# Moving the weighted sum of key products behind the next tile's key eviction on VectorE

## The chip, the cores and the metric

The kernel runs on one core of a Trainium2 chip. A core has a matrix engine (TensorE, PE in the profile; its weight loads are PEld), three elementwise engines (VectorE or DVE, ScalarE or ACT, GpSimd or POOL), a queue that issues transfers (SyncE or SP) and 16 DMA engines. Each engine works through its own instructions in the order in which they stand, and waits for another engine only through semaphores. The metric is the device time of one execution in microseconds (us); lower is better.

## What is computed

One block of a transformer with adaptive layer norms: an attention-like layer, then a mixture of experts, both with residuals. Only the first is touched here. For each of 2 sequences of 1024 tokens of width 512:

```python
h = layernorm(x) * (1 + ca) + sa
Xn = layernorm(h, gamma, beta)
Q, K, V = split(Xn @ W_in + b_in, 3)
K, V = rotary(K), rotary(V)                # on the first 256 of 512 columns
A = sum over tokens of K/|K| * V/|V|       # one row of 512 numbers per sequence
A = 0.5 * A + 0.5
y = (A * Q) @ W_out + b_out + h
x = x + ga * y
```

The row A needs all tokens of its sequence, so nothing of that sequence's output can be computed before its last tile has been added in. Then come a second norm, the choice of 2 of 8 experts for each token, the experts, a shared expert, and the residual. All is in float32.

## The kernel before

The 2048 tokens are 16 tiles of 128, tiles 0 to 7 for the first sequence and 8 to 15 for the second. A tile t passes through these steps:

- `norm1` (L343 to L366): both layer norms. VectorE does the statistics (L311, L312), the reciprocal (L315), the shift and scale (L353, L359) and the offset of the second norm (L322); ScalarE does the square root (L314) and the last scaling into `hn` (L323).
- `turn1` (L368): four transposes on TensorE (L328, `tr_a`), evicted by ScalarE into `xnT` (L375).
- `kv_half(t, 0)` and `kv_half(t, 1)` (L385): four matmuls each into one PSUM bank, keys for 0 and values for 1 (L391). VectorE evicts the bank and adds the bias into half of the tile `kv` (L398). The bank comes from a ring of three (`mm_ps`, L97), which other steps share.
- `kv_back(t, acc)` (L400): ScalarE takes the squares (L408) and the norms (L424). VectorE forms the product of keys and values, `pr` (L410), and the weight `w` = 1/(|K||V|) (L425, L427). GpSimd makes the rotary's part of the product from the same `kv` (L415 to L419); the last of its five instructions writes the tail of `pr`. Then VectorE adds w times `pr`, 768 columns, to the running sum `acc` (L429 for the first tile of a sequence, L431 for the others). That last instruction is the "weighted sum" of this case. The tile `pr` has two buffers, `w` three, `acc` one.

`mix` (L433) turns a finished `acc` into the row A: four small VectorE instructions (L437 to L440), four matmuls with one column (L443, `amix`), two small VectorE instructions. `one_matrix` (L471) folds A into the product of the query and output weights, wp (L496). `project(t, wp)` (L511) then multiplies tile t by it (L522, `o`) and adds the residual on VectorE (L516, L529, L530) and GpSimd (L519); `norm2` (L538) makes `hr` from it, by way of L311, L314, L315, L322 and L323, and `turn2` (L543) transposes `hr` (L328, `tr_c`), evicts it on ScalarE (L550) and scales `hr` on GpSimd (L558, L559).

The first loop (L1044) runs `norm1(t + 2)`, `kv_half(t, 0)`, `turn1(t + 1)`, some side work on the modulation vectors (`side`, L1018), `kv_half(t, 1)` and `kv_back(t)` for tiles 0 to 7. After `mix(0)` and `one_matrix(0)` a plan (L1102) and the list behind it (L1117) interleave `project` of tiles 0 to 7 with the same key and value steps of tiles 8 to 15, the first routing steps (`logits`, `choose`, `ranks`) and chunks of the shared expert. After tile 15 come `mix(1)`, `one_matrix(1)`, `project` of tiles 8 to 15, and from about 345 us on the experts.

The order in the text isn't quite that of the engines: when the program is built, a scheduler sets the order of the instructions on each engine, keeping what depends on what. `tc.issue_after(ins)` tells it to place the instructions of a block behind `ins` on the engine of `ins`.

Of the kernel before, what the change touches and what calls it, by code (L numbers as in the profile page):

```python
# [12 lines left out]
ALU = mybir.AluOpType  # L13
# [11 lines left out]
def kernel(  # L25
# [20 lines left out]
    nc = tc.nc  # L46
    B, S, D = x.shape
# [3 lines left out]
    NJ = S // P  # L51
# [45 lines left out]
    def mm_ps(name):  # L97
        return ps_mm.tile([P, 512], FP, tag="mm", name=name)

    def tr_ps(name):  # L100
        return ps_tr.tile([P, 512], FP, tag="tr", name=name)
# [83 lines left out]
    b_kv = epool.tile([P, 2 * D], FP, name="b_kv")  # L185
# [195 lines left out]
            )  # L381

    fronts = {}

    def kv_half(t, i):  # L385
        g, j = t // 4, t % 4
        if i == 0:
            fronts[t] = kvp.tile([P, 2, D], FP, tag="kv", name=f"kv_{t}")
        ps = mm_ps(f"kv_{t}_{i}")
        for k in range(KC):  # L390
            nc.tensor.matmul(  # L391
                ps,
                xnT[g][:, k, j * P : (j + 1) * P],
                w_kv[:, i, k, :],
                start=(k == 0),
                stop=(k == KC - 1),
            )
        nc.vector.tensor_add(fronts[t][:, i, :], ps, b_kv[:, i * D : (i + 1) * D])  # L398

    def kv_back(t, acc):  # L400

        kv = fronts.pop(t)
        ss = small.tile([P, 2], FP, tag="ss", name=f"ss_{t}")
        sq = kvp.tile([P, D], FP, tag="sq", bufs=1, name=f"sq_{t}")
        for i in range(2):
            nc.scalar.activation(sq, kv[:, i, :], AF.Square, accum_out=ss[:, i : i + 1])  # L408
        pr = kvp.tile([P, D + 2 * R2], FP, tag="pr", name=f"pr_{t}")
        nc.vector.tensor_mul(pr[:, 0:D], kv[:, 0, :], kv[:, 1, :])  # L410
        pair = kv[:, :, 0:ROT].rearrange("p w (i two) -> p w i two", two=2)
        prod = pr[:, 0:ROT].rearrange("p (i two) -> p i two", two=2)
        cross = kvp.tile([P, 2, R2], FP, tag="cross", bufs=1, name=f"cross_{t}")
        both = kvp.tile([P, 2, R2], FP, tag="both", bufs=1, name=f"dsum_{t}")
        nc.gpsimd.tensor_mul(cross[:, 0, :], pair[:, 0, :, 0], pair[:, 1, :, 1])  # L415
        nc.gpsimd.tensor_mul(cross[:, 1, :], pair[:, 0, :, 1], pair[:, 1, :, 0])
        nc.gpsimd.tensor_add(both[:, 0, :], cross[:, 0, :], cross[:, 1, :])
        nc.gpsimd.tensor_sub(both[:, 1, :], prod[:, :, 0], prod[:, :, 1])
        nc.gpsimd.tensor_mul(  # L419
            pr[:, D:].rearrange("p (w i) -> p w i", w=2), both, cs[:, t % NJ]  # L420
        )
        inv = small.tile([P, 2], FP, tag="inv", name=f"inv_{t}")
        nrm = small.tile([P, 2], FP, tag="nrm", name=f"nrm_{t}")
        nc.scalar.activation(nrm, ss, AF.Sqrt)  # L424
        nc.vector.reciprocal(inv, nrm)  # L425
        w = small.tile([P, 1], FP, tag="w", name=f"w_{t}")
        nc.vector.tensor_mul(w, inv[:, 0:1], inv[:, 1:2])  # L427
        if t % NJ == 0:
            nc.vector.tensor_scalar(acc, pr, w, None, ALU.mult)  # L429
        else:  # L430
            nc.vector.scalar_tensor_tensor(acc, pr, w, acc, ALU.mult, ALU.add)  # L431

    def mix(b, acc):  # L433

        pair = acc[:, 0:ROT].rearrange("p (i two) -> p i two", two=2)
        half = kvp.tile([P, 2, R2], FP, tag="cross", bufs=1, name=f"half_{b}")
        nc.vector.tensor_add(half[:, 0, :], pair[:, :, 0], pair[:, :, 1])  # L437
        nc.vector.tensor_add(half[:, 1, :], acc[:, D : D + R2], acc[:, D + R2 :])
        nc.vector.tensor_add(pair[:, :, 0], half[:, 0, :], half[:, 1, :])
        nc.vector.tensor_sub(pair[:, :, 1], half[:, 0, :], half[:, 1, :])  # L440
        ps = tr_ps(f"amix_{b}")
        for f in range(KC):
            nc.tensor.matmul(  # L443
                ps[:, f : f + 1],
                acc[:, f * P : (f + 1) * P],
                ones_t[:, 0:1],
                start=True,
                stop=True,
            )
        aT = small.tile([P, KC], FP, tag="aT", name=f"aT_{b}")  # L450
        RC = ROT // P
        nc.vector.tensor_scalar(
            aT[:, 0:RC], ps[:, 0:RC], 0.5 * (1.0 - HALF), HALF, ALU.mult, ALU.add
        )
        nc.vector.tensor_scalar(
            aT[:, RC:KC], ps[:, RC:KC], 1.0 - HALF, HALF, ALU.mult, ALU.add
        )
        return aT
# [543 lines left out]
    def start_acc(b):  # L1002
        return kvp.tile([P, D + 2 * R2], FP, tag="acc", bufs=1, name=f"acc_{b}")
# [39 lines left out]
    acc = start_acc(0)  # L1043
    for t in range(NJ):  # L1044
        if t == 0:
            norm1_mid(2)
            norm1_out(2)

            nc.vector.scalar_tensor_tensor(
                cs[:, :, 0, :], cs[:, :, 1, :], -2.0, cs[:, :, 0, :], ALU.mult, ALU.mult  # L1050
            )
            nc.vector.scalar_tensor_tensor(
                cs[:, :, 1, :], cs[:, :, 1, :], -2.0, cs[:, :, 1, :], ALU.mult, ALU.mult
            )
            nc.vector.tensor_scalar(cs[:, :, 1, :], cs[:, :, 1, :], 1.0, None, ALU.add)
        else:
            norm1(t + 2)
        kv_half(t, 0)
        turn1(t + 1)
        for step in side[t]:  # L1060
            step()
        kv_half(t, 1)
        kv_back(t, acc)
    kv_half(NJ, 0)
    turn1(NJ + 1)
    kv_half(NJ, 1)
    aT = mix(0, acc)
    norm1(NJ + 2)
    wp = one_matrix(0, aT)
# [24 lines left out]
    def ranks(g):  # L1094
# [5 lines left out]
    acc = start_acc(1)  # L1100
    T = NJ
    plan = {  # L1102
        0: [(kv_back, T, acc), (kv_half, T + 1, 0), (turn1, T + 2)],
        1: [(turn2, 0), (kv_half, T + 1, 1), (kv_back, T + 1, acc)],
        2: [(turn2, 1), (kv_half, T + 2, 0), (turn1, T + 3)],
        3: [(turn2, 2), (kv_half, T + 2, 1), (kv_back, T + 2, acc)],
# [10 lines left out]
    for step, *args in [  # L1117
# [26 lines left out]
        step(*args)  # L1144
    units.close()
    aT = mix(1, acc)
    early.close()
    gbp = ctx.enter_context(tc.tile_pool(name="gbp", bufs=1, reuse_waits="tile"))
# [458 lines left out]
```

## Time and profile before

| | |
|---|---|
| three runs | 793.36, 794.96, 795.88 us; median 794.96 |
| the profiled execution | 793.29 us; its span 791.5 us |
| granted TensorE clock, mean | 0.994 |
| PE busy | 759.0 us, 96% of the span |
| VectorE, ScalarE, GpSimd busy | 426.7, 233.3, 212.0 us |
| L391, matmuls of keys and values | 256 records, 115.3 us |
| L398, their eviction on VectorE | 32, of 658 to 692 ns |
| L431, the weighted sum | 14, of 1017 to 2007 ns |
| L429, the same for the first tile of a sequence | 2, of 611 and 620 ns |
| L419, GpSimd's last instruction before it | 0.72 to 1.05 us |

The span is from the first to the last instruction that the profiler saw; the time of the execution is 1.8 us longer. Percentages over the whole span hide that its stages differ: the keys and values are made from about 19 to 243 us, and the experts, a long stretch in which TensorE has almost no gaps, fill more than half of the rest. A float32 matmul leaves two records, so eight records of L391 are one `kv_half`. In the listing by time, a row gives the start, the duration, engine, line and operation, and in brackets how long the engine sat idle before it and what ended the wait.

### The profile page before, as it was taken

To read this page: it belongs to the slowest core of one execution; us is meant where nothing else is said; L and a number is where in the kernel's file an instruction comes from. 1 tells how busy PE (TensorE), PEld (TensorE's weight loads), DVE (VectorE), ACT (ScalarE), POOL (GpSimd) and SP (SyncE) were. 2 spreads that over 40 slices of the span, in tenths; PEclk is the share of its full clock that TensorE was granted. 3 is DMA by queue.
4 is the path that set the end of the run, shared out by engine and by line. 5 is a ranking of instruction groups with operands and counts; after the bars stand their busy time and mean duration, and the time that the engine had idled before them with its cause. 6 is when DMAs were issued, how large, how long until landed. Compare 5 with 4: busy or idle time off the path is not lost. (4 is left out here: it accounts for less than half of the span.)

```text
span 791.5 us, 8532 instructions
## 1 busy us (share of the span) xinstructions
PE 759.0 (96%) x2547; PEld 418.1 (53%) x2547; DVE 426.7 (54%) x980; ACT 233.3 (29%) x495; POOL 212.0 (27%) x241
## 2 busy tenths in 40 slices
PE   7989999998999978999999999999999999899997
PEld 2433444444444433477466565656566565688542
DVE  4887756788745378897122123323222121489965
ACT  4564532447633046121012112122121121122310
POOL 1233324853621387574200000000000000224530
PEclk9999999999999999999999999999999999999999
DMA  9940001211435520247999999999999976624551
GB/s 324 384 143 28 0 1 66 107 45 49 160 93 173 212 106 27 81 176 248 363 324 328 325 335 334 336 340 327 326 332 333 335 248 232 197 85 120 162 170 53
DMA packets 96369, 158.91 MB, mean 201 GB/s; under 512 B 8089, under 2 KB 51097, under 8 KB 96321
## 3 DMA queue, kind: packets, MB, share of 16 engines
q1 hardware_dynamic: 89984, 138.41, 51.7%
q0 software_dynamic: 5760, 18.88, 7.2%
q10 hardware_dynamic: 576, 1.05, 0.4%
q8 instruction: 22, 0.36, 0.2%
q14 instruction: 27, 0.21, 0.1%
HBM read 128.15 MB, written 30.16 MB: 200 GB/s over the span
## 5 line engine op out<-in xcount | busy, mean ns | idle before, releaser
L1259 POOL DMA_INDIRECT y<-ybuf,yrows x32 | 37.0, 1157 | 334.4 <-SPq L1485 287.1
L391 PE MATMUL kv<-w_kv,xnT 128*128 128x512 f32 x256 | 115.3, 597 | 4.6 <-DVE kv L398 2.5
L1385 PE MATMUL by<-wd_r,gtT 128*128 128x512 f32 (+1 forms) x210 | 96.1, 593 | 0.9 <-DVEq L1477 0.9
L1357 PE MATMUL bg<-wg_r,hbT 128*128 128x352 f32 x280 | 88.9, 460 | 0.9 <-ACT y L1389 0.9
L1357 PE MATMUL bu<-wu_r,hbT 128*128 128x352 f32 x280 | 88.5, 459 | 0.0
L391 PEld LDWEIGHTS kv<-w_kv,xnT 128*128 128x128 f32 x256 | 47.0, 190 | 62.0 <-issue 49.0
L1357 PEld LDWEIGHTS bu<-wu_r,hbT 128*128 128x128 f32 x280 | 53.2, 190 | 29.6
L1372 DVE COPY gtT<-gtr 128x256 f32<-128x256 f32 x35 | 14.9, 425 | 97.0 <-PE gtr L1369 97.0
L1357 PEld LDWEIGHTS bg<-wg_r,hbT 128*128 128x128 f32 x280 | 50.4, 190 | 23.5 <-ACT y L1389 1.3
L522 PE MATMUL o<-wp,xnT 128*128 128x512 f32 x128 | 58.4, 602 | 0.0
L1385 PEld LDWEIGHTS by<-wd_r,gtT 128*128 128x128 f32 (+1 forms) x210 | 37.2, 191 | 34.6 <-issue 33.5
L1236 DVE TENSOR_TENSOR sg_b<-sg_b,bg 128x352 f32<-128x352 f32 x35 | 18.2, 521 | 68.8 <-ACT sg_b L1235 68.8
L1349 ACT COPY hbT<-tr_b 128x512 f32<-128x512 f32 x36 | 21.1, 586 | 101.1 <-PE tr_b L328 101.1
L1237 DVE TENSOR_TENSOR gt<-sg_b,bu 128x352 f32<-128x352 f32 x35 | 18.3, 521 | 47.2 <-PE bu L1357 47.2
L1389 ACT COPY y<-by 128x512 f32<-128x512 f32 x35 | 20.5, 587 | 70.8 <-DMA wg_r<-in_w_gate_dram 35.7
L522 PEld LDWEIGHTS o<-wp,xnT 128*128 128x128 f32 x128 | 24.4, 195 | 29.2 <-issue 27.5
L573 POOL DMA_INDIRECT hbuf<-again,rows x24 | 25.6, 1068 | 50.5 <-DMA again<-hlin 24.3
L1235 ACT ACTIVATE sg_b<-bg 128x352 f32<-128x352 f32 x35 | 16.2, 464 | 76.1 <-PE bg L1357 76.1
L415 POOL TENSOR_TENSOR cross<-kv 128x128 f32<-128x128 f32 x16 | 12.7, 791 | 82.1 <-DVE kv L398 49.6
L408 ACT ACTIVATE sq<-kv 128x512 f32<-128x512 f32 x32 | 20.1, 629 | 35.0 <-DVE kv L398 31.2
L496 PE MATMUL wp<-aw,wqT 128*128 128x512 f32 x64 | 28.3, 597 | 0.9 <-DVE aw L480 0.8
L519 POOL TENSOR_TENSOR x<-x,sa 128x512 f32<-128x512 f32 x16 | 20.3, 1269 | 31.5 <-DVE sa L508 15.6
(315 smaller groups left out, 1269.7 us busy)
## 6 DMA issues: line engine op xcount, KB each, us to landing
wg_r<-in_w_gate_dram SPq DMA_DIRECT2D x35, 704.0 KB, 6.1
wu_r<-in_w_up_dram SPq DMA_DIRECT2D x35, 704.0 KB, 7.5
wd_r<-in_w_down_dram SPq DMA_DIRECT2D x35, 512.0 KB, 5.6
hb<-hbuf SPq DMA_DIRECT2D x36, 256.0 KB, 5.0
ybuf<-y SPq DMA_DIRECT2D x31, 256.0 KB, 5.4
wd_r<-in_w_down_dram SPq DMA_DIRECT2D x35, 192.0 KB, 5.4
wmod<-in_wmod_dram SPq DMA_DIRECT2D x6, 1024.0 KB, 9.9
x<-in_x_dram SPq DMA_DIRECT2D x3, 1024.0 KB, 10.5
```

Of the source, the lines that this page charges most:

```text
L391: nc.tensor.matmul(ps, xnT[g][:, k, j * P : (j + 1) * P], w_kv[:, i, k, :], start=(k == 0), stop=(k == KC - 1),)
L408: nc.scalar.activation(sq, kv[:, i, :], AF.Square, accum_out=ss[:, i : i + 1])
L496: nc.tensor.matmul(ps, wqT[:, k, f * P : (f + 1) * P], aw[:, k, :], start=(k == 0), stop=(k == KC - 1),)
L519: nc.gpsimd.tensor_add(xt, xt, sg[b])
L522: nc.tensor.matmul(ps, xnT[g][:, k, j * P : (j + 1) * P], wp[:, k, :], start=(k == 0), stop=(k == KC - 1),)
L573: ins = nc.gpsimd.indirect_dma_start(out=hbuf, out_offset=bass.IndirectOffsetOnAxis(ap=idx, axis=0), in_=src, in_offset=None, bounds_check ...
L1237: nc.vector.tensor_mul(dst, sg[:m, :n], pu[:m, :n])
L1259: nc.gpsimd.indirect_dma_start(out=y, out_offset=None, in_=ybuf, in_offset=bass.IndirectOffsetOnAxis(ap=yrows[:, t, s : s + 1], axis=0), b ...
L1349: nc.scalar.copy(hbT.rearrange("p k q -> p (k q)"), ps)
L1357: nc.tensor.matmul(ps[:, :H], hbT[:, k, :], wt[:, k, :], start=(k == 0), stop=(k == KC - 1))
L1385: nc.tensor.matmul(ps, gtT[:m, c, :], w[2][:m, c, :], start=(c == 0), stop=(c == NH - 1))
L1389: nc.scalar.copy(y, ps)
```

## The change

```diff
     fronts = {}
+    waiting = []
...
-        nc.vector.tensor_add(fronts[t][:, i, :], ps, b_kv[:, i * D : (i + 1) * D])
+        ins = nc.vector.tensor_add(
+            fronts[t][:, i, :], ps, b_kv[:, i * D : (i + 1) * D]
+        )
+        if i == 0 and waiting:
+
+            with tc.issue_after(ins.ins):
+                waiting.pop()()
...
-        if t % NJ == 0:
-            nc.vector.tensor_scalar(acc, pr, w, None, ALU.mult)
-        else:
-            nc.vector.scalar_tensor_tensor(acc, pr, w, acc, ALU.mult, ALU.add)
+
+        def accumulate():
+            if t % NJ == 0:
+                nc.vector.tensor_scalar(acc, pr, w, None, ALU.mult)
+            else:
+                nc.vector.scalar_tensor_tensor(acc, pr, w, acc, ALU.mult, ALU.add)
+
+        waiting.append(accumulate)
 
     def mix(b, acc):
 
+        if waiting:
+            waiting.pop()()
```

`kv_back` no longer issues the weighted sum; it leaves it in a list. The next `kv_half(t, 0)`, the keys of the next tile, issues it directly behind its own eviction. For the last tile of the second sequence there is no next tile, and `mix` issues it, where it stood before. No instruction is added or taken away.

What this makes of the order on the engines, in the built program:

| place | VectorE before | VectorE after |
|---|---|---|
| tile 1 | w, sum 1, offset (L322), keys 2, reciprocal | w, offset, reciprocal, keys 2, sum 1 |
| tile 3 | w, sum 3, keys 4, side step (L258), offset, reciprocal, side step | w, offset, keys 4, sum 3, two side steps, reciprocal |
| tile 7 | w, sum 7, keys 8, mix | w, offset, keys 8, sum 7, mix |
| tile 8 | sum 8 inside `one_matrix` | keys 9, sum 8 |
| tile 9 | w, sum 9, L529 to L322 of projection 2, keys 10 | w, L529 to L322 of projection 2, keys 10, sum 9 |
| tile 11 | w, reciprocal, sum 11, offset, L529 of projection 6 | w, reciprocal, offset, L529 of projection 6; the sum much later, behind keys 12 |

("keys t" is the eviction L398 of `kv_half(t, 0)`.) The other tiles go like these. TensorE keeps its order but for one tile: matmuls of `kv_half(2, 1)` and four groups of transposes of the query weights (L466) mix in another way. ScalarE has a few square roots, norms and evictions exchanged with their neighbours. GpSimd has one place, at tile 12, where the five instructions of L415 to L419 come ahead of two others (L999 and L1000) instead of between and behind them. SyncE keeps its order.

## Prediction

> **What bounds the kernel.** I read the page's busy line first, then the chain that ended last, then the list of who waited for whom on PE.
>
> ```profile
> PE 759.0 (96%) x2547; PEld 418.1 (53%) x2547; DVE 426.7 (54%) x980; ACT 233.3 (29%) x495; POOL 212.0 (27%) x241
> ...
> PE m L961 8%; PE sd L873 5%; PE ph L1244 1%; DVE spare_again L1288 0%; DVE spare_again L1289 0%
> ```
>
> TensorE is busy for 759.0 of 791.5 us and the chain's long pieces are TensorE's. No matmul is removed, so the change can win only gaps of TensorE: 32.5 us in all, and only those before the last weighted sum at 243.7 us that come from VectorE's order. By stretches of 10 us the granted clock is 1.00 as far as 250 us, so no clock is to be gained there. From 400 to 600 us PE is busy for 100.0 of each 100 us: work that starts earlier there should end earlier by as much.
>
> ```profile
> PE tr_c L328 <- ACT hr L323: 8.8, 7, 4.6
> PE kv L391 <- DVE kv L398: 2.5, 2, 1.7
> PE kv L391 <- ACT xnT L375: 2.1, 3, 1.0
> ...
> PE wqT L466 <- ACT xnT L375: 1.4, 1, 1.4
> ...
> PE amix L443 <- DVE acc L440: 1.2, 1, 1.2
> ```
>
> Columns: total us, times, longest. These five lines are my candidates; the largest wait of the first line, 4.6 us at 281, lies behind the last weighted sum (there L530 waits 5.4 us for GpSimd's L519) and is not one.
>
> **Where the wait sits.** VectorE by time, around tile 4:
>
> ```profile
> 62.82 0.16 DVE L312 BATCH_NORM_AGGREGATE mv<-st_a 128x2 f32<-128x6 f32 x1
> 64.54 1.02 DVE L431 SCALAR_TENSOR_TENSOR acc<-pr,w,acc 128x768 f32<-128x768 f32 x1 [1.56 <-POOL pr L419]
> 65.48 0.68 DVE L398 TENSOR_TENSOR kv<-kv,b_kv 128x512 f32<-128x512 f32 x1
> ```
>
> and TensorE in the same stretch:
>
> ```profile
> 55.16 7.13 PE L391 MATMUL kv<-w_kv,xnT 128*128 128x512 f32 x16 [0.81 <-DVE kv L398]
> 62.13 0.60 PE L328 MATMUL tr_a<-ident,hn 128*128 128x128 f32 x4
> 62.66 1.88 PE L252 MATMUL modsum<-wmod,pick 128*2 128x512 f32 x4
> 66.22 7.13 PE L391 MATMUL kv<-w_kv,xnT 128*128 128x512 f32 x16 [1.68 <-DVE kv L398]
> ```
>
> The keys of tile 4 were complete at about 62.2, but VectorE stood before the weighted sum of tile 3, which waited for GpSimd until 64.5, took 1.02, and only then evicted them. The bank was needed again (three banks, two of them with the side step), so TensorE stood 1.68 us. Over all weighted sums VectorE idled 15.2 us for L419, but a wait of VectorE costs only where TensorE stands behind it.
>
> **Part 1, the eviction goes in front (tiles 0 to 6).** No cost: the same instructions. The eviction takes 0.66 to 0.69 in all 32 cases and fills the wait (0.58 to 1.65 us a tile up to tile 7). At tile 4 it can start at 63.0 to 63.2 and end by 63.9, before TensorE wants the bank at 64.54; at tile 3 it ends by 54.1 (a statistic, 0.66, is now ahead of it too), wanted at 54.35. So the two waits of L391 go: 0.81 + 1.68 = **2.5 us**. Between: 1.7 if tile 3's bank is late, 2.5 at most.
>
> **Part 2, the offset no longer behind the sum.** At tile 1 the offset L322 ran at 42.72, after the sum; by the new order it can run at 40.8, so `hn` (42.97) and the three evictions of `xnT` behind it (to 44.83), which held TensorE for 1.39 us, come nearly 2 us sooner. But TensorE's own order there changes: two matmul records of the 8 now stand ahead of the transposes instead of four, so it arrives 0.95 us sooner. The two gaps there, 1.39 + 0.27, become about 0.9 + 0.35: gain **0.4**, bounds -0.3 and 1.4.
>
> **Part 3, `mix(0)`.** L443 waits 1.19 us for L440. If the sum of tile 7 still starts at 100.73, when L419 is done, the four instructions of `mix` no longer have the eviction (0.60 from start to start) ahead of them: 0.6. The earlier offset of tile 6 (94.11, now about 91.7) also frees the eviction of tile 7's values, at 96.36 although TensorE had finished them near 94.8; with it GpSimd's five start earlier. Taken **1.0**, at most 1.2.
>
> **Part 4, tiles 8 to 15.** The sum of tile 9 and what stood behind it:
>
> ```profile
> 137.81 0.25 DVE L427 TENSOR_TENSOR w<-inv 128x1 f32<-128x1 f32 x1
> 139.78 2.01 DVE L431 SCALAR_TENSOR_TENSOR acc<-pr,w,acc 128x768 f32<-128x768 f32 x1 [1.72 <-POOL pr L419]
> 141.72 0.73 DVE L529 SCALAR_TENSOR_TENSOR u<-u,rs,o 128x512 f32<-128x512 f32 x1
> ```
>
> L529 had its matmul at about 138.2, and waited 3.5 us in VectorE's queue. From L529 to `hr` (145.76) are 4.0 us, and `tr_c` stood 0.62 us for it. Now L529 starts near 138.3. The same holds at 154.93 (`tr_c` waits 0.36) and 172.72 (1.04). Sum 2.02. The moved sum takes 1.0 to 2.0 us behind the keys' eviction, where VectorE waited 1.5 to 3 us for `o` anyway; without that cover it would lengthen the next `hr` by as much.
>
> [...] What used to idle until L419 now runs L530 and L516, both with two SBUF inputs, against L419, L558 and L559. [...]
>
> ```profile
> 197.50 6.93 DVE L410 TENSOR_TENSOR pr<-kv 128x512 f32<-128x512 f32 x1
> ```
>
> It let six GpSimd instructions in a row pass: 6.3 us lost. By that row L530 would get in only after L559, near 142.4, where it ran before (142.49), and part 4 would bring nothing. [...] The eviction itself has one input in PSUM and showed no lengthening beside L519 at 145.64 and 150.75, so parts 1 and 3 don't hang on this.
>
> **Part 5, further down.** Because the offset at 174.65 no longer waits for the sum of tile 11, ScalarE's `hn` (174.88), then the exponential and its table loads up to 184.7 come 1.8 to 3.4 us sooner; TensorE, about 1 us sooner itself, stood 0.54 + 1.00 for `xnT` of tile 12: half of it, **0.7** (0 to 1.5). The wait of `lg` at 210.1 (0.63) follows the offset at 207.92, which also moves ahead of its sum: **0.3** (0 to 0.6). `mix(1)` gains nothing: its sum ends at 244.7, `amix` runs in TensorE's order at 249.7.
>
> Behind this, DMA waits on buffers that TensorE frees, and GpSimd's scatters wait for row numbers from the matmuls at 250.5; both move with TensorE. The sum: 2.5 + 0.4 + 1.0 + 1.7 + 0.7 + 0.3 = 6.6. I take off 1.0 for new small gaps where TensorE, now earlier, catches up with ScalarE (estimate: the size of one `xnT` wait): **5.6 us**. The profiled execution took 793.29 (span 791.5 and 1.8 around it), so 787.7; it lay 1.67 below the median of the three runs. Against the median: 794.96 - 5.6 = **789.4**.
>
> **Rivals.** A measurement tells 0.3%, 2.4 us, from no change.
>
> A, only the first stage gains (parts 1 to 3, 2.5 to 3.9 us; part 4 lost to GpSimd): about 791.5. [...] 20%.
>
> B, no effect: TensorE's gaps move. The per-tile chain norm, transpose, `xnT` is as long as TensorE's 8.8 us a tile, and what is won at 54 and 64 is lost at the next `tr_a`. Against: VectorE is busy 6.6 to 8.4 of each 10 us from 40 to 100, and `hn` at 66.90 is wanted at 73.2. Also here: the scheduler's other exchanges cost what the gaps bring. About 794.5. 17%.
>
> C, slower, one mechanism: GpSimd keeps VectorE out. If L530 or L516, now inside GpSimd's run, loses 6.3 us as L410 did, `hr` comes 6.3 - 3.5 = 2.8 us later than before. At the three places of part 4 that is 8.4, less the 3.9 of the first stage: 799.5. It is slower from about two such places on (5.6 against 3.9). For: the row. Against: GpSimd's runs there are three instructions, not six. 12%.
>
> The forecast has 51%, its own range 786.8 to 791. Faster by over 0.3% (below 792.6): 51 and most of A, 68%. Same: 20%, B and the weak end of A. Slower: 12%. For 8 in 10: from 786.8, all bounds at their good end, to 795, which takes in A and most of B.
>
> **What would show it.** Part 1: the list of PE's waits has no L391 waiting for L398. Part 2: less than 1.3 us at L466. Part 3: L443's wait below 0.4. Part 4: `tr_c` waits for `hr` no more between 140 and 190, and L530 stays below 2 us. Part 5: L391 waits for `xnT` less than 1 us. PE's idle time falls from 32.5 to about 27. I am wrong if L431's wait for L419 vanishes and PE's idle time stays, or if a VectorE instruction of several us stands in front of an `hr`.

## The result, and the profile after

The change makes the kernel faster, by more than was forecast. Six executions of the changed kernel have a median of **786.11 us** (783.34 to 788.17). Six of the kernel before, run beside them, have 796.14 (793.36 to 797.12). The ratio is 0.988, with a 95% interval of 0.985 to 0.991. The forecast was 789.4 us with a range from 786.8: the sign is right, the gain is too small, and the measured time lies 0.7 us below the range. Chance can have a part in those 0.7 us: when both kernels ran again (`e1_before` and `e2_after` below), the changed one had a median of 788.46, inside the range, and the gain by medians was 7.5 us instead of 10.0. That the parts of the sum were too small together isn't chance; the ledger below shows it place by place.

The profiled execution took 788.17 us, with a span of 786.2. The page's busy line:

```profile
PE 760.1 (97%) x2547; PEld 420.3 (53%) x2547; DVE 428.1 (54%) x980; ACT 232.6 (30%) x495; POOL 212.8 (27%) x241
```

TensorE has the same 2547 records and is busy for the same time within 1.1 us. Its idle time fell from 32.5 to 26.1 us, so most of the gain is in its gaps, as forecast. The list of who waited for whom on TensorE (engine, tile and line, released by; total us, times, longest):

```profile
PE tr_c L328 <- ACT hr L323: 6.9, 4, 4.5
PE kv L392 <- ACT xnT L375: 3.3, 2, 2.8
```

Of the five lines shown of before, those for `kv` behind VectorE's eviction, for `wqT` and for `amix` no longer occur, and `tr_c` went from seven waits to four. One line grew: `xnT` from 2.1 to 3.3. (The new lines 399, 426, 440, 542 and 543 are 398, 419, 431, 529 and 530 of before, and the matmul of keys and values is L392. The kernels of the experiments have line numbers of their own; the tile's name tells what a row is.)

VectorE and TensorE around tile 4, by time:

```profile
60.86 0.21 DVE L322 TENSOR_SCALAR off_b<-mv_b,rs_b 128x1 f32<-128x1 f32 x1
60.99 0.68 DVE L399 TENSOR_TENSOR kv<-kv,b_kv 128x512 f32<-128x512 f32 x1
62.47 1.02 DVE L440 SCALAR_TENSOR_TENSOR acc<-pr,w,acc 128x768 f32<-128x768 f32 x1 [0.80 <-POOL pr L426]
```

```profile
59.94 1.88 PE L252 MATMUL modsum<-wmod,pick 128*2 128x512 f32 x4
61.75 7.13 PE L392 MATMUL kv<-w_kv,xnT 128*128 128x512 f32 x16
```

The eviction of the keys (L399) stands ahead of the sum. VectorE still waits for GpSimd's `pr`, 0.80 us, but with nothing behind it that TensorE needs: the next matmuls follow the side step with no bracket. Over the whole run VectorE's wait for `pr` fell from 15.2 to 1.9 us, because other work now fills it.

For the second sequence, the stretch of tile 9 on VectorE:

```profile
131.90 0.26 DVE L434 TENSOR_TENSOR w<-inv 128x1 f32<-128x1 f32 x1
132.37 0.75 DVE L542 SCALAR_TENSOR_TENSOR u<-u,rs,o 128x512 f32<-128x512 f32 x1 [0.22 <-PE o L535]
133.23 1.15 DVE L543 TENSOR_TENSOR x<-x,u 128x512 f32<-128x512 f32 x1
...
136.84 0.68 DVE L399 TENSOR_TENSOR kv<-kv,b_kv 128x512 f32<-128x512 f32 x1
137.44 1.80 DVE L440 SCALAR_TENSOR_TENSOR acc<-pr,w,acc 128x768 f32<-128x768 f32 x1
```

L542, which stood 3.5 us in VectorE's queue before, now finds the queue free and itself waits 0.22 us for `o`. The residual's addition L543 takes 1.15 us beside GpSimd, and the sum 1.80, but the sum now lies where no matmul waits for it.

**A ledger by place.** How much sooner does the same TensorE work start? I compare the profile of before with a second profile of the changed kernel (the run `e2_after` below), since in neither of them does the granted clock drop between 20 and 250 us. The first keys start 0.14 us apart (18.57 and 18.71).

| TensorE work | before, us | change, us | gained since the row above | forecast |
|---|---|---|---|---|
| side step (L240) ahead of the keys of tile 3 | 52.42 | 50.67 | 1.75 | 0.4 (part 2) |
| values of tile 4 | 66.22 | 61.83 | 2.64 | 2.5 (part 1) |
| `amix` of the first sequence | 103.33 | 97.60 | 1.34 | 1.0 (part 3) |
| router product `lg`, group 0 | 170.80 | 163.55 | 1.52 | 1.7 (part 4, with the next row) |
| `tr_c` of tile 6 | 183.20 | 174.75 | 1.20 | |
| `rank` | 191.35 | 183.79 | -0.89 | 0.7 (part 5) |
| `lg`, group 1 | 210.11 | 201.76 | 0.79 | 0.3 (part 5) |
| first wp of the second sequence | 251.43 | 242.97 | 0.11 | -1.0 (the allowance) |

Together 8.46 us by 243 us, where 5.6 were forecast. From the first keys to that wp TensorE's idle time fell from 10.5 to 3.7 us and its busy time from 222.4 to 220.6, with 659 records in both; why a gap cost more than its idle time here is told under part 3 below. The spans of these two profiles, 791.5 and 781.8, differ by 9.7; the other 1.2 us arise behind 243 and I don't assign them to a step.

### The profile page after: what moved, and what is told of

Same layout as the page of the kernel before. It is cut to its first block, busy times and chain, and to the rows that moved or that the text cites. A ratio compares the mean times of both kernels' runs of the same rounds, so it can differ in the third digit from the quotient of the medians.

```text
span 786.2 us, 8525 instructions
## 1 busy us (share of the span) xinstructions
PE 760.1 (97%) x2547; PEld 420.3 (53%) x2547; DVE 428.1 (54%) x980; ACT 232.6 (30%) x495; POOL 212.8 (27%) x241
## 5 line engine op out<-in xcount | busy, mean ns | idle before, releaser
L392 PE MATMUL kv<-w_kv,xnT 128*128 128x512 f32 x256 | 116.7, 603 | 3.3 <-ACT xnT L375 3.3
L392 PEld LDWEIGHTS kv<-w_kv,xnT 128*128 128x128 f32 x256 | 47.6, 192 | 61.3 <-issue 49.4
L415 ACT ACTIVATE sq<-kv 128x512 f32<-128x512 f32 x32 | 20.2, 630 | 33.2 <-DVE kv L399 29.0
L399 DVE TENSOR_TENSOR kv<-kv,b_kv 128x512 f32<-128x512 f32 x32 | 21.9, 683 | 13.2 <-PE kv L392 13.0
```

The source lines that it names most:

```text
L392: nc.tensor.matmul(ps, xnT[g][:, k, j * P : (j + 1) * P], w_kv[:, i, k, :], start=(k == 0), stop=(k == KC - 1),)
L399: ins = nc.vector.tensor_add(fronts[t][:, i, :], ps, b_kv[:, i * D : (i + 1) * D])
```

## The experiments

Each kernel ran beside the kernel before on the same chip. In the profiles, "20 to 250" is the stretch before wp of the second sequence.

**Both kernels again (`e1_before`, `e2_after`), unchanged.** One profile of each is little to build a ledger on.

> The kernel before, once more, for a second profile of it. The two profiles at hand differ by 5.3 us in span but the timed runs by 10. Theory G (the gain lies in TensorE's waits up to 250 us, and the rest of the difference is halved-clock stretches that come and go between executions): the first wp matmul of the second sequence starts at 251 to 252 us as before, and this span differs from 791.5 only by whole stretches of about 3.4 us at clock 0.50, each worth 1.7 us. Rival H (something behind 250 us got faster): the span is 794 or more with no more halved stretches than the three of the first profile. Ratio 0.998 to 1.002.

> The changed kernel, once more. Theory G: the first wp matmul of the second sequence starts at 243 to 245 us, TensorE again waits 2 to 3 us for xnT of tile 12 near 178, and where that wait is followed by a stretch at clock 0.50 the start is 1.7 us later than where it is not. Rival H: it starts at 244.5 and the span is below 783 with the same number of halved stretches as in the first profile (four). Ratio 0.985 to 0.991.

The kernel before: 796.25 us, ratio 0.9998 (0.998 to 1.001). The change: 788.46 (783.51 to 791.3), ratio 0.990 (0.988 to 0.993). The gain repeats. In the repeat of before, wp of the second sequence started at 252.73 rather than 251.43, although its waits in the stretch were those of the first profile but for 0.5 us more at `lg`. The profile has a half-clock stretch at 104 us, of the kind told of in the last section, and such a stretch cost 1.70 or 1.71 us wherever one lay by itself ahead of the end of the run. So starts are compared only between profiles without one ahead of them, or with 1.7 us taken off for each.

**Only the first sequence, only the second (`e3_first_seq`, `e4_second_seq`).** Rival A said that only the first stage gains.

```diff
-        waiting.append(accumulate)
+        if t < NJ:                    # second kernel: t >= NJ
+            waiting.append(accumulate)
+        else:
+            accumulate()
```

> Only the sums of tiles 0 to 7 are deferred; tiles 8 to 15 issue theirs at once, as before. Theory G: the first profile's gains at wqT, keys 3 and 4 and amix stay (1.8 + 2.6 + 1.4 = 5.8 us by 104 us), the three tr_c waits for hr between 140 and 190 are back (2.0 us), and the wait for xnT of tile 12 is the 1.5 us of before without a halved stretch; 250 us is reached 5.5 to 6.5 us sooner: ratio 0.9915 to 0.9935. Rival (the change works as one, each stage needs the other): below 3 us, ratio above 0.996.

> Only the sums of tiles 8 to 15 are deferred; tiles 0 to 7 as before. Theory G: the waits at wqT, keys 3 and 4 and amix are those of before (5.4 us), the three tr_c waits are gone (2.6 us with what else moves), and the new wait for xnT of tile 12 (2.75 instead of 1.54 us) with its halved stretch takes back 1.2 to 2.9: 250 us is reached 0.5 to 3 us sooner, ratio 0.996 to 0.9995. Rival (GpSimd and VectorE keep each other out, so that the second sequence gains nothing): tr_c waits again for hr, and 250 us is reached later than before.

First sequence alone: 788.19 us, ratio 0.991 (0.988 to 0.994). Second alone: 793.6, ratio 0.998 (0.996 to 0.999). The two gains, 0.91% and 0.24%, add to 1.15%, and the whole change gave 0.96% and 1.21% in its two comparisons: within the noise the halves add up, and most of the gain is the first sequence's. wp of the second sequence starts 5.4 us sooner than before with the first sequence alone (246.07; the expectation had 5.5 to 6.5). With the second alone it starts at 253.82 behind three half-clock stretches, which is 2.7 us sooner when 5.1 are taken off for them. TensorE's waits of 1 us and more from 20 to 250 us, first sequence alone:

```profile
PE tr_c L328 <- ACT hr L323: 2.0, 3, 1.0
PE kv L392 <- ACT xnT L375: 1.5, 2, 1.0
PE lg L621 <- ACT lgps L613: 1.1, 1, 1.1
```

and second alone:

```profile
PE kv L392 <- ACT xnT L375: 2.7, 1, 2.7
PE kv L392 <- DVE kv L399: 2.5, 2, 1.7
PE wqT L482 <- ACT xnT L375: 1.4, 1, 1.4
PE amix L459 <- DVE acc L456: 1.1, 1, 1.1
```

Of the waits of before, each takes away those of its own half and leaves the others. The second also shows where the long `xnT` wait comes from: it is there with tiles 8 to 15 changed and not with tiles 0 to 7 changed.

**The eviction or the offset (`e5_offset_only`, `e7_offset_tile1`, `e8_evict_first`).** In the change two things of VectorE pass the sum: the eviction of the next keys, and in some tiles the offset L322. Which brings the gain?

The first attempt asked the scheduler to place the sum behind the offset of tile t+2:

```diff
+        with ExitStack() as behind_off:
+            if f"b{t + 2}" in offs:
+                behind_off.enter_context(tc.issue_after(offs[f"b{t + 2}"].ins))
```

> The kernel before, with each weighted sum of tiles 0 to 7 placed behind the offset (L322) of the tile two ahead, but still in front of the next tile's key eviction. Theory G splits the change into two moves. If so, what hangs on the offset is won here: the wait at wqT (1.39 + 0.27) goes, 1.8 us. What hangs on the eviction stays: keys 3 and keys 4 wait 0.8 and 1.7 for L398 (less at tile 3 if its offset pulls anything along), amix still waits 0.6 to 1.2, and tiles 8 to 15 are as before. wp of the second sequence starts 1.7 to 2.5 us sooner, ratio 0.9965 to 0.9985. Rival (all hangs on the eviction; the offset only follows): no wait of before goes, ratio 0.999 to 1.001.

794.67 us, ratio 0.9998 (0.9985 to 1.0010), with the same waits as before but for 0.5 us more at `lg`. The edit was void: that offset already stood in front of the sum, since the scheduler runs a tile further ahead than the loop; it is the offset of tile t+3 that followed. It says nothing on the question.

The second placed the offset ahead of the sum and kept the sum ahead of the eviction. VectorE's order differs from that of before at tile 1, the place of part 2, and in exchanges that the scheduler made just behind it (among them, the eviction of tile 2's values now stands behind a shift for a later tile, L353 of before):

```diff
+        with ExitStack() as first:
+            if i == 0 and waiting:
+                off = offs.get(f"b{t + 2}") or offs[f"b{t + 1}"]
+                with tc.issue_after(off.ins):
+                    s = waiting.pop()()
+                first.enter_context(tc.issue_after(s.ins))
```

> The kernel before, with one change of order on VectorE: at tile 1 the offset L322 stands ahead of the weighted sum; the eviction of keys 2 stays behind the sum, and all other sums stay ahead of the next keys. Theory G: the wait at wqT (1.39 + 0.27 us, 1.8 us of time) goes, because it hangs on the offset alone; keys 3 and keys 4 still wait for L398, amix still for L440. wp of the second sequence starts at 249 to 250 us where no halved stretch lies ahead of it. Rival (the wait at wqT hangs on the eviction or on TensorE's new order): the wait stays above 1.2 us. The time itself is near what 3 rounds can tell: ratio 0.996 to 0.999.

795.83 us, ratio 1.0014 (1.0005 to 1.0022): nothing gained. TensorE in its profile:

```profile
43.36 1.13 PE L487 MATMUL wqT<-ident,w_q 128*128 128x128 f32 x8 [0.61 <-ACT xnT L379]
45.99 0.66 PE L487 MATMUL wqT<-ident,w_q 128*128 128x128 f32 x4 [0.63 <-ACT wqT L490]
...
55.80 1.55 PE L396 MATMUL kv<-w_kv,xnT 128*128 128x512 f32 x3 [1.72 <-DVE kv L409]
```

The two waits at `wqT` fell from 1.39 and 0.27 to 0.61 and 0.63, in sum 0.4 us, where the expectation had them gone. The wait for the next eviction of keys grew from 0.81 to 1.72. TensorE came to it 0.26 us sooner, and the eviction, still behind its sum, came 0.65 us later (55.07 instead of 54.42), since the values' eviction that was exchanged started at 49.76 instead of 48.65. `amix` started at 103.98, not sooner than before's 103.33. A gap was moved, not closed: rival B's mechanism, for this part alone. The 0.65 us belong to the exchange and not to the offset, so the run shows that an offset moved by itself brought nothing here, not that it must.

The third did the opposite: in tiles 0 to 7 eviction, sum, offset, in that order; `norm1` of tile t+2 is also asked for later, behind `kv_half(t, 0)`.

```diff
+            if name[0] == "b" and 3 <= int(name[1:]) <= NJ + 1 and sums:
+                later.enter_context(tc.issue_after(sums[-1].ins))
...
-        else:
-            norm1(t + 2)
...
+        if t:
+            norm1(t + 2)
```

> Tiles 0 to 7: the eviction of the next keys stands ahead of the weighted sum, and the offset that the change had put ahead of both stays behind the sum; to have it there the norm of tile t + 2 is asked for behind the matmuls of keys t. Tiles 8 to 15 as before. Theory G: keys 3 and keys 4 do not wait (2.6 to 2.8 us won), amix waits about 0.6 less, and the wait at wqT stays within 0.5 us of 1.66. wp of the second sequence 2.5 to 4 us sooner than before, ratio 0.995 to 0.998. Rival (the offset pulls all else along; the eviction alone does little): keys 3 and 4 still wait over 1 us in sum.

789.56 us (four executions), ratio 0.993 (0.990 to 0.996), and:

```profile
44.15 1.13 PE L489 MATMUL wqT<-ident,w_q 128*128 128x128 f32 x8 [0.15 <-ACT wqT L492]
...
98.26 1.05 PE L466 MATMUL amix<-ones_t,acc 128*128 128x1 f32 x8 [0.36 <-DVE acc L463]
```

`amix` at 98.26 is 5.1 of the 5.7 us that the change gains there, and no matmul of keys waits for an eviction any more. So the waits of part 1 hang on the eviction's place, and the offset need not pass the sum for them to go. The gain is larger than expected (0.995 to 0.998), and the reason is a part that was missed, the wait at `wqT`, 0.15 where some 1.7 was expected: with the norm asked for later, ScalarE's `hn` came to stand behind the four `xnT` evictions instead of among them. So this kernel changes two things at that place. Neither run splits the 1.75 us that the change gains there between the offset and the eviction.

**The long wait for `xnT` (`e6_norm_late`).** Part 5 had the wrong sign. ScalarE at tile 12 in the first profile of the change:

```profile
175.43 0.79 ACT L563 ACTIVATE hT<-tr_c,modT 128x128 f32<-128x128 f32 x2
178.77 0.29 ACT L314 ACTIVATE sd_b<-mv_b,eps_t 128x1 f32<-128x1 f32 x1 [2.55 <-DVE mv_b L312]
178.97 0.79 ACT L563 ACTIVATE hT<-tr_c,modT 128x128 f32<-128x128 f32 x2
179.66 0.80 ACT L375 ACTIVATE xnT<-tr_a,colsb 128x128 f32<-128x128 f32 x2
```

A square root of 0.29 us for tile 13 stands between two pairs of evictions and waits 2.55 us for statistics on VectorE; TensorE waits 2.75 us for the evictions behind it. In the kernel before it stood later, between the first and the other three `xnT` evictions, and waited less:

```profile
186.03 0.47 ACT L375 ACTIVATE xnT<-tr_a,colsb 128x128 f32<-128x128 f32 x1
187.98 0.29 ACT L314 ACTIVATE sd_b<-mv_b,eps_t 128x1 f32<-128x1 f32 x1 [1.48 <-DVE mv_b L312]
188.18 1.14 ACT L375 ACTIVATE xnT<-tr_a,colsb 128x128 f32<-128x128 f32 x3
```

The experiment is the change with the norm of tile 13 asked for one step later in the plan:

```diff
-        6: [(turn2, 5), (choose, 0), (chunk, 0), (norm1, T + 5)],
-        7: [(turn2, 6), (turn1, T + 4), (kv_half, T + 4, 0), (ranks, 0)],
+        6: [(turn2, 5), (choose, 0), (chunk, 0)],
+        7: [(turn2, 6), (turn1, T + 4), (norm1, T + 5), (kv_half, T + 4, 0), (ranks, 0)],
```

> The changed kernel with one more edit: the norm of tile 13 is asked for behind the transposes of tile 12 instead of ahead of them, so that its square root no longer stands among ScalarE's evictions for tile 12. Theory: the new 2.75 us wait for xnT of tile 12 falls below 1.2 us and no stretch at clock 0.50 follows it; wp of the second sequence starts at 240.5 to 241.8 instead of 243.0. Ratio to the kernel before 0.985 to 0.989, about 2 us better than the change alone. Rival: the norm of tile 13 is then late itself and TensorE waits as long for its transposes or at the next keys; no better than the change.

**782.04 us** (779.83 to 785.39), ratio 0.982 (0.980 to 0.985): more than expected (0.985 to 0.989), and this version beats both kernels, though it ran beside the kernel before only and not beside the change. TensorE's matmuls for that tile, and all of its waits from 20 to 250 us:

```profile
177.37 3.73 PE L392 MATMUL kv<-w_kv,xnT 128*128 128x512 f32 x8
```

```profile
PE wp L509 <- DVE aw L493: 0.7, 2, 0.4
PE wp L509 <- ACT aw L489: 0.3, 1, 0.3
```

1.0 us of waiting is left in this stretch. wp of the second sequence starts at 240.11, 2.86 us sooner than in the second profile of the change. The edit moves the whole norm of tile 13, its statistics on VectorE too; it doesn't move the square root alone. Of these 2.86 about 1.4 remain at 290 us, since a `tr_c` near 270 then waits 6.38 us for `hr` instead of 4.91 (VectorE waited at that place for GpSimd's part of the residual, 5.38 us in the profile of before and 5.31 in the first of the change).

## Why the prediction was right in its mechanism and wrong in its size

**What bounds the kernel: right.** TensorE's idle time was forecast at 27 us and came to 26.1, and to 26.4 in the second profile. The error is in the sizes. Against the forecast by places the ledger has 1.35 us more for part 2, 1.02 more for part 4, 1.11 for the allowance that wasn't needed, 0.97 more for the smaller rest, and 1.59 less for part 5 at `xnT`: 2.86 in all. That the total isn't further off is in part luck, since part 5 failed the other way.

**Part 1 (2.5): right.** L392 no longer waits for the eviction; 2.64 us measured. The first-sequence run shows that it doesn't need the rest of the change, and `e8_evict_first` that the eviction's place does it.

**Part 2 (0.4): the largest of the gains that were put too low.** The stretch brought 1.75 us, and both waits at `wqT` went. The step that failed is "by the new order it can run at 40.8", a start read from the times of before. The offset and `hn` before, in `e7_offset_tile1`, and in the change:

```profile
42.72 0.21 DVE L322 TENSOR_SCALAR off_b<-mv_b,rs_b 128x1 f32<-128x1 f32 x1
42.97 0.81 ACT L323 ACTIVATE hn<-h,off_b,rs_b 128x512 f32<-128x512 f32 x1 [1.54 <-DVE off_b L322]
...
40.84 0.21 DVE L324 TENSOR_SCALAR off_b<-mv_b,rs_b 128x1 f32<-128x1 f32 x1
41.12 0.80 ACT L327 ACTIVATE hn<-h,off_b,rs_b 128x512 f32<-128x512 f32 x1
...
39.87 0.21 DVE L322 TENSOR_SCALAR off_b<-mv_b,rs_b 128x1 f32<-128x1 f32 x1
40.15 0.80 ACT L323 ACTIVATE hn<-h,off_b,rs_b 128x512 f32<-128x512 f32 x1
```

`e7_offset_tile1` is the case that the working describes, and there the working came out: the two gaps were forecast at 0.9 + 0.35 and measured 0.61 + 0.63, almost the same sum. In the change VectorE also skips the wait of tile 0's sum (0.58 us) and reaches tile 1 about 0.85 us sooner, so that the evictions behind `hn` ended at 42.34, against 43.31 in that run and 44.83 before. I had counted that TensorE arrives sooner, and not that VectorE does. The forecast's own sign, a wait at L466 below 1.3, was met by far.

**Part 3 (1.0): right in kind, 1.34 measured.** Its upper bound was 1.2, the idle time of L443 and a little. Here and elsewhere a wait cost more than its idle time. `amix` starts 4.78 us after the previous product with a wait of 1.19 and 3.43 without: 1.35 us. The keys of tile 3 start 2.74 us after the side step with 0.81 of waiting and 1.85 without: 0.89. In these rows a matmul that waits for nothing starts before the modelled end of the one before it, and one that waits doesn't. By these rows and that of `tr_c` (4.22 with 0.62 of waiting, 3.44 without: 0.78), 0.08 to 0.16 us a wait are missing from the bounds that I took from idle time alone.

**Part 4 (1.7): right that it survives GpSimd; 2.72 measured to `tr_c` of tile 6.** The three waits of 2.02 us in sum were worth about 2.5, for the reason given under part 3, so its upper bound of 2.0 was too low as well. No run shows the 1.7 in the sum: it was my estimate of what GpSimd would leave of the 2.02. In its place the runs showed this. Before, the sum L431 took 2.00 or 2.01 us at the three places where L558 had started 0.07 or 0.08 us ahead of it, and 1.02 at the other eleven; the difference lies in the row's own time and not in a wait ahead of it. After, L530 (now L543) stayed at 0.69 to 1.51 us over its eight places up to 179 us, and GpSimd's L571 (L558 of before), next to the row of 1.15 us above, took 1.72 instead of 1.27. The row of 6.93 us didn't recur (the longest of its kind, L417, now takes 2.23, at the place where GpSimd's own order changed too): rivals A and C fell with that. The second-sequence run measures the part with part 5 at 0.24% (0.10 to 0.38), 1.9 us.

**Part 5 (0.7 + 0.3): wrong sign at `xnT`.** -0.89 measured up to `rank`. I reasoned that the chain ahead of `xnT` starts sooner, and looked at the moved exponential and its table loads only. I had noted that ScalarE has "a few square roots, norms and evictions exchanged with their neighbours", and priced none. One was this square root, which now waited 2.55 us ahead of the evictions. The run that moved the norm took the wait away and gained about 0.6% more than the change alone (782.04 against medians of 786.11 and 788.46 in other comparisons).

**The 1.0 us taken off: not there as small gaps.** From 20 to 250 us the lists have two new waits, the square root's and one of 0.27 us at wp of the first sequence, where another fell from 0.52 to 0.37. The same 1.0 was left in the range's low end. The good ends of the five parts sum to 2.5 + 1.4 + 1.2 + 2.0 + 1.5 + 0.6 = 9.2, and 794.96 - 9.2 = 785.8 would have held the measured 786.11, narrowly.

## What to carry to other kernels

In an in-order queue, put the instruction that frees another engine's buffer ahead of the one that waits for a third engine: here doing so with fifteen evictions of 0.68 us was worth about 1% of the kernel. When an order changes, compute the new starts of both engines, since the engine that was stuck comes forward too. Then look through every neighbour that the scheduler exchanged: a square root of 0.29 us that came to stand among evictions went with a wait of 2.75 us on TensorE.

## What the runs showed of the hardware

**A half-clock stretch behind short waits.** After TensorE's 2.75 us wait for `xnT`, the same eight matmuls took 5.40 us in the first profile of the change and 3.70 in the second:

```profile
180.16 5.40 PE L392 MATMUL kv<-w_kv,xnT 128*128 128x512 f32 x8 [2.75 <-ACT xnT L375]
```

```profile
180.25 3.70 PE L392 MATMUL kv<-w_kv,xnT 128*128 128x512 f32 x8 [2.75 <-ACT xnT L375]
```

The first profile by stretches of 1 us (length, then busy us and instructions of PE, PEld, DVE, ACT and POOL, then the granted clock, DMA share and GB/s):

```profile
180.00:181.00 1.00, 0.84 (x2) 0.49 (x3) 0.97 (x5) 1.00 (x3) 0.00 (x0) 1.00 0.00 0
181.00:182.00 1.00, 1.00 (x3) 0.45 (x2) 0.90 (x3) 1.00 (x5) 0.00 (x0) 0.69 0.00 0
182.00:183.00 1.00, 1.00 (x2) 0.38 (x2) 0.93 (x4) 0.84 (x3) 0.00 (x0) 0.50 0.00 0
183.00:184.00 1.00, 1.00 (x2) 0.33 (x1) 0.96 (x3) 0.20 (x1) 0.00 (x0) 0.50 0.00 0
184.00:185.00 1.00, 1.00 (x3) 0.36 (x2) 0.53 (x1) 0.00 (x0) 0.00 (x0) 0.60 0.00 0
```

The clock falls to 0.50 and the missing parts, 0.31 + 0.50 + 0.50 + 0.40, are 1.71 us lost over some 3.4 us. All such stretches of the ten profiles of this case, but for the end of the run:

| wait of TensorE ahead of it | followed by a half-clock stretch |
|---|---|
| 0.8 to 1.2 us at `tr_a` and 0.55 at `kv` behind it, about 18 us | 1 of 10 |
| 2.75 us at `xnT`, 180 to 190 us | 2 of the 3 profiles that have it |
| 0.4 to 1.2 us at `amix` and 0.3 to 0.5 at wp behind it, about 100 us | 4 of 6 |
| no wait at `amix` there | 0 of 4 |
| 4.5 to 6.4 us at `tr_c`, 270 to 284 us | all 10, once or twice |
| 0.9 to 1.3 us at `tr_c` and `rank`, 300 to 320 us | 5 of 10 |
| 0.8 to 0.9 us at `by` and 2.0 at `m` 5 us later, 664 to 680 us | 6 of 10 |

In slices of 1 us these stretches look alike: the clock falls to 0.50, and each loses 1.70 or 1.71 us (3.41 or 3.42 for two that follow on each other, between 270 and 290 us). By these rows the waits ahead need not be long: 2.75 us, and 1.2 + 0.3 us with only one-column matmuls and four transposes between, were followed by a drop in some of the profiles. This is a correlation over ten profiles; no run here changed such a wait alone.

The profiles have two to five such stretches ahead of the end of the run, a spread of 5 us. It can be part of why single executions of one kernel lie up to 5 us from their median, and it is most of why the first profiles of before and after have spans 5.3 us apart where the medians differ by 10: the first of the change has two such stretches, at 181 and 672, which the first of before hasn't. If the rows are more than chance, a removed wait is worth more than its idle time for this reason too; that isn't shown here.
